# Silu through Tanh, paired value blocks and a detached last linear in a two-block macaron kernel

## The chip, the core and the metric

The kernel runs on one core of a Trainium2 chip. The metric is the time of one execution on the device in microseconds, taken as the median of several runs. The profiles come from the hardware profiler, one execution each.

## The reference

The input x has 16 batches of 256 rows of 128 features, all float32. One feed-forward, a cheap attention, the same feed-forward again, and then a mixture of experts, a real attention and the mixture of experts again are added to x one after the other, each on the layer-normed x:

```
x = x + 0.5 * ffn(norm(x))              # which = 0
x = x + nonlocal_attention(norm(x))     # no softmax: three small products per batch
x = x + 0.5 * ffn(norm(x))              # which = 1, same weights
x = x + 0.5 * experts(norm(x))          # 2 of 8 experts of rank 64 by the first row of each batch
x = x + attention(norm(x))              # 16 heads of 8, rotary, causal, softmax
x = x + 0.5 * experts(norm(x))

ffn(x):  h = silu(x w1 * s1) * (x w2 * s2)     # 128 -> 512
         h = gelu(h h1 * s_h1)                 # 512 -> 512, exact gelu
         h = gelu(h h2 * s_h2)                 # 512 -> 512
         return h w3 * s3                      # 512 -> 128
```

## The kernel before

x stays in on-chip memory the whole time. The 16 batches form nine groups (`BATCHES`): seven of two batches and two of one. Each group passes the two feed-forwards and the attention blocks; the unit of work of a feed-forward is one group, so 512 columns for the large groups and 256 for the small ones.

**The order of work is planned when the kernel is built.** Every piece of work is a Python generator, called a line. It yields a `step` before each operation: the engine, an assumed duration, the PSUM banks and buffers it takes and drops, the results it needs. A loop at the end of the kernel keeps a clock for each engine, picks the line that can begin first, issues its operation and advances the clock. The instructions of an engine are pinned in that order (`Ordered`, the helper at line 227, so nearly all instructions carry that line in the profile). The planner runs once; on the chip each engine runs its list in order and waits on semaphores.

- `main` is the line of `feed_forwards`: it goes through `order`, in which the two feed-forwards of different groups alternate, and issues the matmuls of each with their full 128*128 tiling. While feed-forwards remain, other lines go first on TensorE when they are ready (`back`), and `main` fills the rest.
- In a feed-forward (`ffn`) the first stage makes, for each of four chunks of the 512 hidden features, one matmul with `w1T` into a bank `pu` and one with `w2T` into a bank `pw`. The line `silu` reads `pu` on ScalarE and drops the bank; `product` multiplies on VectorE with `pw` and the scale `s2` and writes `h`. The two 512 x 512 layers follow in seven block products each instead of eight (Strassen), whose operand differences `T` run on VectorE or POOL and whose sums `h<-h,pb` run on VectorE, then Gelu on ScalarE. The last linear, `w3s`, is issued by `main` itself, in two halves; after it `main` goes to the next feed-forward.
- After a feed-forward other lines are spawned: `nonlocal_attn` after the first, `experts`, `attention` and `after_attention` after the second.
- `attention` makes score blocks with four matmuls side by side in 32 rows each (tiling 32*128 in the profile, `pb<-qkv`), once for the row maxima (`maxima`, VectorE's TENSOR_REDUCE `mx`) and once for the exponentials (`weighted`). A score block takes four PSUM banks (a quad). `softmax` runs Exp on ScalarE into a buffer `pr` (three of them) and POOL zeroes what lies above the diagonal. The heads are four quarters, `j` = 0, 2, 1, 3. `values` takes one quarter at a time: 16 matmuls in the tiling 128*32 (`pb<-pr,vm`) on `pr`, which it then drops. In the last two groups (`late`) the result is given on in halves.
- The flag `ended` is set when `main` has issued the last feed-forward. From then on the planner may use all banks, adds the mask of the scores on TensorE, and puts matmuls of the identity (`pb<-ident`) into idle stretches of TensorE to keep its clock up (`awake`).
- `either` steps may run on one of two engines; `pick` takes the one that would be done first by the planner's clocks, with `SPARED` added for VectorE. `LOAN` makes the first four banks dearer, `PATIENCE` delays an exponential that needs a table load, `SLACK` is the span of time within which candidates count as equally early.

ScalarE needs a table for its functions, and the program loads another where the function needs it (ACT_TABLE_LOAD).

The scales `s1` and `s2` come in on POOL's DMA queue. The first group's layer norm (`first_input`) uses POOL for one power (`rstd`).

Of the kernel before, what the change touches and what calls it, by code (L numbers as in the profile page):

```python
# [20 lines left out]
P = 128  # L21
# [6 lines left out]
LANDING = 2.2  # L28
LOAN = 1.5
SPARED = 0.5  # L30
PATIENCE = 1.5
HURRY = 1
SLACK = 0.02
HOP = {"PE": 0.24, "ACT": 0.15, "DVE": 0.12, "POOL": 0.08}
# [23 lines left out]
def macaron_kernel(ctx: ExitStack, tc: tile.TileContext, a: dict, out: bass.AP):  # L58
# [30 lines left out]
    warm = cst.tile([P, 1], F32, name="warm")  # L89
    nc.scalar.activation(warm, ident[:, :1], AF.Silu)  # L90
    for _ in range(WARM):
        nc.tensor.matmul(pb[:, 7, :P], ident, ident, start=True, stop=True)
    s1 = load("s1", [P, KC], a["s1"], nc.gpsimd)
    s2 = load("s2", [P, KC], a["s2"], nc.gpsimd)

    rot = cst.tile([P, 4, TG], F32, name="rot")
# [278 lines left out]
    def ffn(which, t0, n):  # L375
        me, N = (which, t0), n * P
        xnT = xnTs.pop(me)
        h = None

        def silu(c, pu, sil):  # L380
            yield act(N, table="silu", drop=(pu,), sets=(("s", c, me),))
            nc.scalar.activation(sil[:, :N], pu.t[:, :N], AF.Silu, scale=s1[:, c : c + 1])

# [71 lines left out]
        for c in range(KC):  # L455
            r = yield pe(0.215 * n, banks=1, after=0.0, take=("h",) if c == 0 else ())
            h = r[1] if c == 0 else h
            pu = r[0]
            nc.tensor.matmul(pu.t[:, :N], w1T[:, c * P : (c + 1) * P], xnT.t[:, :N], start=True, stop=True)
            sil = sml.tile([P, TG], F32, name="sil", bufs=3)  # L460
            spawn(silu(c, pu, sil))
            (pw,) = yield pe(0.215 * n, banks=1, after=0.0, drop=(xnT,) if c == KC - 1 else ())
            nc.tensor.matmul(pw.t[:, :N], w2T[:, c * P : (c + 1) * P], xnT.t[:, :N], start=True, stop=True)
            spawn(product(c, pw, sil, h))
            if me == (0, 0) and c == 1:
                fold_w3()
        lo, hi = 0, 2 * P
        for l, w in ((1, h1T), (2, h2T)):
# [9 lines left out]
            for p, b, first, at, second, needs in (  # L478
# [9 lines left out]
                for o in range(2):  # L488
                    for k in range(2):
                        begins, ends = o + k == 0, o + k == 2  # L490
                        drop = ()
                        if ends and p in (5, 7, 4):
                            drop = (T[{5: 1, 7: 3, 4: 4}[p]],) + ((h,) if p == 4 else ())
                        r = yield pe(
                            0.1075 * n, banks=int(new and begins), after=0.0, take=("h",) if p == 1 and begins else (),
                            needs=needs, drop=drop, sets=(("P6", l, me),) if p == 6 and ends else (),
# [20 lines left out]
                elif p == 4:  # L517
                    spawn(other_block(l, 1, 0, bk["c"], nh))
            h = nh

        half = n // 2
        po = {}
        up, down = (0, 1, 2, 3), (2, 3, 0, 1)
        for t, ks in [(t, down) for t in range(half, n)] + [(t, up) for t in range(half)]:
            new = t in (0, half)
            last = t in (half - 1, n - 1)
            r = yield pe(
                0.225 * len(ks), banks=int(new), after=0.0, needs=tuple((2, i, t // half, me) for i in range(2)),
                drop=(h,) if t == half - 1 else (),
            )  # L530
            if new:
                po[t // half] = r[0]
            b = po[t // half]
            for k in ks:
                nc.tensor.matmul(
                    b.t[:, t % half * P : (t % half + 1) * P], h.t[:, k, t * P : (t + 1) * P], w3s[:, k, :],
                    start=(k == ks[0]), stop=(k == ks[-1]),
                )
            if last:
                spawn(residual(t // half, b))  # L540

# [10 lines left out]
    def nonlocal_attn(t0, n):  # L552
# [19 lines left out]

        gram = yield from product(0.45 * nb, None, None, "gram", (xn,))
        m = yield from product(0.22 * nb, gram, pht, "gph")
        m = yield from product(0.22 * nb, m, wgT, "eff")
        if t0 == 2 * FIRST[NG - 1]:
            spawn(for_the_mask())
        (po,) = yield pe(0.45 * nb, banks=1, drop=(xnT,))
        for t in range(n):
# [7 lines left out]
    def gated(nb, cls):  # L587

        (bk,) = yield pe(0.22 * nb, banks=1)
        pl = bk.t[:, : nb * NE].rearrange("p (b e) -> p b e", e=NE)  # L590
# [32 lines left out]
        for b in range(nb):  # L623
            scaled_by(ab.t[:, b, D:], ab.t[:, b, D:], gw[:, b : b + 1])
        (bk,) = yield pe(0.23 * nb, banks=1, drop=(ab,))
        pw = bk.t[:, : 2 * D].rearrange("p (b d) -> p b d", b=2)
# [11 lines left out]
    def applied(key, sg, xnT):  # L638
        yield step(None, 0.0, needs=(key,))
        we = merged[key]  # L640
        (po,) = yield pe(0.225 * sg.n, banks=1, drop=(we, xnT) if sg.last else (xnT,))
        for t in range(sg.n):
            nc.tensor.matmul(
                po.t[:, t * D : (t + 1) * D], xnT.t[:, t * P : (t + 1) * P], we.t[:, t // 2, :], start=True, stop=True
            )
        yield dve(sg.n * P, drop=(po,))
        add_residual(sg.t0, sg.n, po)
# [55 lines left out]
    def attention(sg):  # L703
# [6 lines left out]
        if sg.first:  # L710

            (bk,) = yield pe(0.22 * nb, banks=1)
            py = bk.t[:1, : 2 * D].rearrange("p (b d) -> p b d", b=2)
# [33 lines left out]
        spawn(queries())  # L747
        (bk,) = yield pe(0.225 * n, banks=1, needs=(("q", sg.t0),), drop=(xnT,))
        pv = bk.t.rearrange("p (t d) -> p t d", d=D)
# [75 lines left out]
        def weighted(i):  # L825
# [55 lines left out]
            def values():  # L881

                po = [None, None]
                for j in (0, 2, 1, 3):
                    new = j == 0 or (late and j == 1)
                    yield step(None, 0.0, needs=(("pr", sg.t0, i, j), ("v", sg.t0)))
                    pr = prs[j]
                    r = yield pe(0.025 + 0.00174 * o, banks=int(new), tiles="col", drop=(pr,))
                    if new:
                        po[j % 2 :] = [r[0]] * (2 - j % 2)  # L890
                    half = slice((j % 2) * w, (j % 2) * w + w)
                    pp = po[j % 2].t[:, half]
                    for k, f, at in runs:
                        for r in range(4):
                            nc.tensor.matmul(
                                pp[32 * r : 32 * r + 32, (f - q0) * P :], vm.t[:, base // P + k, r, j, :],
                                pr.t[:, r, at : at + (q1 - f) * P],
                                start=(j < 2 and k == 0), stop=(j >= 2 and k == q1 - 1), skip_group_check=True,
                            )
                    if late and j >= 2:  # L900
                        spawn(output(pp, oT[:, half], w // 32, j % 2, po[j % 2], ("oT", sg.t0, i, j)))
                    elif j == 3:
                        spawn(output(po[0].t[:, : 2 * w], oT[:, : 2 * w], w // 16, 0, po[0], ("oT", sg.t0, i, j)))
# [204 lines left out]
    def feed_forwards():  # L1108

        for which, sg in order:  # L1110
# [13 lines left out]
            if (which, sg) == order[0]:  # L1124
                fold_rest()
        ended[0] = True

# [9 lines left out]
    while lines:  # L1137
# [4 lines left out]
        back = engine == "PE" and begun[0] <= len(order) - HURRY  # L1142
        line = min(soon, key=lambda r: ((r[2] is main) == back, r[2].rank, r[1]))[2]
        issue(line)
# [71 lines left out]
```

## Time and profile before

| | |
|---|---|
| median of 3 runs | 934.62 us (934.36 to 934.98) |
| the profiled execution | 934.55 us |
| its span, first to last instruction | 932.8 us |
| mean granted TensorE clock | 0.996 |
| TensorE busy | 904.2 us (97%) |
| VectorE busy | 636.3 us (68%) |
| ScalarE busy | 471.5 us (51%), of it 110.3 us table loads |
| POOL busy | 356.4 us (38%) |
| first matmul of the first and of the last feed-forward | 8.6 and 817.5 us |
| last matmul of the last feed-forward's last linear | 845.2 us |

In a row of the profile's groups, the names left of the arrow are written and those right of it read, buffer numbers left out; `pb` is the whole of PSUM. Behind the bar stand the busy time in us, the mean of one in ns, the idle time of the engine just before these instructions, and what ended most of it. A timeline row gives start, duration and engine, and merges neighbours of one kind (x16). A float32 matmul appears as two instructions. DMA traffic matters at the start alone: the weights and x come in during the first 30 us.

### The profile page before, as it was taken

Reading aid. Unit: us, or ns where it says so; the run is one execution under the profiler, and the core shown is the slowest. Engines: PE = TensorE matmul, PEld = TensorE weight load, DVE = VectorE, ACT = ScalarE, POOL = GpSimd, SP = SyncE. Lnnn points to the kernel's source line nnn. Section 1 sums busy time; section 2 is a strip of 40 time slices with the busy share of each in tenths; the row PEclk is TensorE's granted clock in tenths of the full one; section 3 lists DMA queues with packets and bytes.
Section 4 is the critical chain, followed back from the end, with each engine's and each line's share of the span. In section 5 each row is a group of like instructions: output and inputs, shape, how many; then the busy total and the mean of one; then the engine's idle time right before and its main releaser. Section 6 shows DMA issues by size and latency. Waiting matters only on the chain.

```text
span 932.8 us, 16458 instructions
## 1 busy us (share of the span) xinstructions
PE 904.2 (97%) x6524; PEld 680.5 (73%) x6524; DVE 636.3 (68%) x1474; ACT 471.5 (51%) x691; POOL 356.4 (38%) x537
## 2 busy tenths in 40 slices
PE   6999999999999999999999999999999989999998
PEld 4778778686786767787677767866786767877666
DVE  4744646875488485894678764894778586977773
ACT  2233533645754646546555466547574657465332
POOL 5311313522454334442453324532463246443441
PEclk9999999999999999999999999999999999999999
DMA  8100000000000000000000000000000000000000
GB/s 240 33 1 1 1 1 12 12 1 1 13 12 12 1 2 12 24 1 1 12 1 24 1 1 13 24 1 1 13 2 23 1 12 1 25 7 2 13 19 12
DMA packets 14588, 13.68 MB, mean 15 GB/s; under 512 B 2032, under 2 KB 11952, under 8 KB 14512
## 3 DMA queue, kind: packets, MB, share of 16 engines
q1 hardware_dynamic: 12496, 8.04, 3.0%
q0 software_dynamic: 1600, 4.20, 1.6%
q8 instruction: 51, 0.84, 0.4%
q10 hardware_dynamic: 416, 0.39, 0.1%
q14 instruction: 25, 0.20, 0.1%
HBM read 10.53 MB, written 2.10 MB: 14 GB/s over the span
## 4 chain that ended last, share of the span: by engine, by line
PE 70%; DVE 14%; ACT 6%; issue 4%; POOL 2%; DMA 2%; SPq 1%; POOLq 0%; DVEq 0%
PE pb L227 70%; DVE mx L227 4%; DVE h L227 3%; ACT L227 2%; ACT pr L227 2%; DVE pb L227 2%; DMA w3s<-in_w3T_dram 1%; ACT h L227 1%; POOL pr L227 1%; DVE T L227 1%; DMA x<-in_x_dram 1%; DVE st L227 1%; DVE qkv L227 1%; POOL rstd L227 1%; DVE row L227 0%
## 5 line engine op out<-in xcount | busy, mean ns | idle before, releaser
L227 DVE TENSOR_TENSOR h<-h,pb 128x512 f32<-128x512 f32 (+1 forms) x180 | 111.7, 620 | 80.8 <-PE pb L227 78.8
L227 PE MATMUL pb<-T,hS 128*128 128x256 f32 (+1 forms) x576 | 131.8, 364 | 3.9 <-DVE h L227 2.8
L227 POOL TENSOR_SCALAR_AFFINE_SELECT pr<-pr 128x512 f32<-128x512 f32 x128 | 78.8, 639 | 140.4 <-ACT pr L227 135.3
L227 ACT ACTIVATE h<-h 128x512 f32<-128x512 f32 (+1 forms) x108 | 62.3, 581 | 137.7 <-DVE h L227 137.3
L227 ACT ACTIVATE pr<-pb 128x1536 f32<-128x1536 f32 x64 | 92.7, 1449 | 54.0 <-PE pb L227 40.4
L227 PE MATMUL pb<-qkv 32*128 32x256 f32 (+2 forms) x1536 | 115.2, 406 | 4.7 <-ACT pr L227 2.5
L227 ACT ACT_TABLE_LOAD x86 | 110.3, 1283 | 17.8 <-PE pb L227 15.5
L227 DVE TENSOR_REDUCE mx<-pb 128x8 f32<-128x2048 f32 (+1 forms) x64 | 111.9, 1750 | 6.1 <-PE pb L227 5.7
L227 PEld LDWEIGHTS pb<-T,hS 128*128 128x128 f32 x576 | 96.5, 190 | 21.1 <-issue 8.6
L227 DVE TENSOR_TENSOR pb<-pb,causal 128x1024 f32<-128x1024 f32 x56 | 68.7, 1226 | 45.4 <-PE pb L227 37.3
L227 PEld LDWEIGHTS pb<-qkv 32*128 32x128 f32 x1536 | 68.0, 184 | 38.3 <-issue 11.4
L227 ACT ACTIVATE xn<-x,shift,rstd 128x128 f32<-128x128 f32 x138 | 57.1, 482 | 52.9 <-POOL shift L227 52.7
L227 POOL TENSOR_SCALAR nm<-mv 128x4 f32<-128x4 f32 (+3 forms) x56 | 14.8, 264 | 168.3 <-DVE mv L227 167.1
L227 POOL TENSOR_TENSOR T<-h 128x512 f32<-128x512 f32 (+1 forms) x48 | 53.4, 1112 | 58.9 <-ACT h L227 54.9
L227 POOL TENSOR_TENSOR T<-h,T 128x512 f32<-128x512 f32 (+1 forms) x40 | 46.1, 1151 | 64.9 <-DVE h L227 35.0
L227 PE MATMUL pb<-xnT,w1T 128*128 128x512 f32 (+1 forms) x144 | 68.9, 560 | 0.9 <-ACT xnT L227 0.9
L227 PE MATMUL pb<-xnT,w2T 128*128 128x512 f32 (+1 forms) x144 | 68.2, 555 | 1.0 <-ACT sil L227 0.8
L227 PE MATMUL pb<-h,h1T 128*128 128x256 f32 (+1 forms) x288 | 68.8, 364 | 0.0
L227 POOL TENSOR_TENSOR rstd<-ve,mhalf 128x4 f32<-128x4 f32 (+3 forms) x63 | 58.9, 935 | 24.9 <-DVE ve L227 20.1
L227 PE MATMUL pb<-h,h2T 128*128 128x256 f32 (+1 forms) x288 | 67.1, 364 | 0.0
L227 PE MATMUL pb<-T,h1T 128*128 128x256 f32 (+1 forms) x288 | 66.1, 359 | 0.0
L227 PEld LDWEIGHTS pb<-w3s,h 128*128 128x128 f32 x512 | 60.6, 192 | 7.0 <-issue 6.0
(138 smaller groups left out, 1568.9 us busy)
## 6 DMA issues: line engine op xcount, KB each, us to landing
out_dram<-x SPq DMA_DIRECT2D x7, 256.0 KB, 2.3
x<-in_x_dram SPq DMA_DIRECT2D x6, 256.0 KB, 5.3
h1T<-in_h1T_dram SPq DMA_DIRECT2D x1, 1024.0 KB, 9.6
h2T<-in_h2T_dram SPq DMA_DIRECT2D x1, 1024.0 KB, 11.0
ab<-in_eab_dram,at POOLq DMA_INDIRECT x32, 2.9
x<-in_x_dram SPq DMA_DIRECT2D x3, 128.0 KB, 5.4
w1T<-in_w1T_dram SPq DMA_DIRECT2D x1, 256.0 KB, 3.5
w2T<-in_w2T_dram ACTq DMA_DIRECT2D x1, 256.0 KB, 3.9
```

The lines of the kernel that those rows point to most:

```text
L227: return lambda *args, **kw: tc.keep_in_program_order(getattr(self.engine, name)(*args, **kw))
```

## The change

Silu(u) is computed as u (1 + tanh(u / 2)) / 2. The two halves are put into the scales: `s1` is halved and `s2` multiplied by the halved `s1`, on POOL, after their load. ScalarE writes Tanh of the scaled bank, and a new VectorE operation makes (tanh + 1) times the bank; the bank is dropped after that. The planner counts Tanh to Gelu's table, and the first table loaded is Gelu's.

`values` takes the quarters 0 and 2 in one step and 1 and 3 in another, but for late groups. The last linear becomes a line of its own with the rank of `main`; `main` goes on, and sets `ended` when the last feed-forward's residuals are added. While TensorE is in one of the tilings, candidates of a tiling go before untiled ones. The planner's assumed times of TensorE and five of its constants change.

```
-LOAN = 1.5
-SPARED = 0.5
-PATIENCE = 1.5
+LOAN = 2.0
+SPARED = 0.1
+PATIENCE = 1
-SLACK = 0.02
+SLACK = 0.05
...
-    nc.scalar.activation(warm, ident[:, :1], AF.Silu)
+    nc.scalar.activation(warm, ident[:, :1], AF.Gelu)
...
     s1 = load("s1", [P, KC], a["s1"], nc.gpsimd)
     s2 = load("s2", [P, KC], a["s2"], nc.gpsimd)
+    nc.gpsimd.tensor_scalar(s1, s1, 0.5, None, ALU.mult)
+    nc.gpsimd.tensor_tensor(s2, s2, s1, ALU.mult)
...
         def silu(c, pu, sil):
-            yield act(N, table="silu", drop=(pu,), sets=(("s", c, me),))
-            nc.scalar.activation(sil[:, :N], pu.t[:, :N], AF.Silu, scale=s1[:, c : c + 1])
+            yield act(N, table=soft)
+            nc.scalar.activation(sil[:, :N], pu.t[:, :N], AF.Tanh, scale=s1[:, c : c + 1])
+            yield dve(N, drop=(pu,), sets=(("s", c, me),))
+            nc.vector.scalar_tensor_tensor(sil[:, :N], sil[:, :N], 1.0, pu.t[:, :N], ALU.add, ALU.mult)
...
-            r = yield pe(0.215 * n, banks=1, after=0.0, take=("h",) if c == 0 else ())
+            r = yield pe(0.015 + 0.215 * n, banks=1, after=0.0, take=("h",) if c == 0 else ())
...
-        half = n // 2
+        def last_linear(h=h):
...
-            r = yield pe(
-                0.225 * len(ks), banks=int(new), after=0.0, needs=tuple((2, i, t // half, me) for i in range(2)),
+                r = yield pe(
+                    0.237 * len(ks), banks=int(new), after=0.0, needs=tuple((2, i, t // half, me) for i in range(2)),
...
+        spawn(last_linear(), since=0.0)
...
-                for j in (0, 2, 1, 3):
-                    new = j == 0 or (late and j == 1)
-                    yield step(None, 0.0, needs=(("pr", sg.t0, i, j), ("v", sg.t0)))
-                    pr = prs[j]
-                    r = yield pe(0.025 + 0.00174 * o, banks=int(new), tiles="col", drop=(pr,))
+                for js in ((0,), (2,), (1,), (3,)) if late else ((0, 2), (1, 3)):
+                    new = js[0] == 0 or (late and js[0] == 1)
+                    yield step(None, 0.0, needs=tuple(("pr", sg.t0, i, j) for j in js) + (("v", sg.t0),))
+                    r = yield pe(
+                        (0.025 + 0.00174 * o) * len(js), banks=int(new), tiles="col", drop=tuple(prs[j] for j in js)
+                    )
...
+        yield step(None, 0.0, needs=tuple(("ffn", h, (1, order[-1][1].t0)) for h in range(2)))
         ended[0] = True
...
-        line = min(soon, key=lambda r: ((r[2] is main) == back, r[2].rank, r[1]))[2]
+        inside = engine == "PE" and tiles[0] is not None
+        line = min(
+            soon, key=lambda r: (inside and r[2].next["tiles"] is None, (r[2] is main) == back, r[2].rank, r[1])
+        )[2]
```

The other changed lines set the assumed time of a 128-column matmul pair to 0.237 us (from 0.22 to 0.23) and add 0.015 us to each step of the feed-forward.

## The prediction

> **What bounds the kernel now.** I read the busy rows of the page first, then the table of stretches, then the waits of TensorE inside one stretch, and last the timeline, since a share of 97% does not say whether the rest can be had.
>
> ```profile
> PE 904.2 (97%) x6524; PEld 680.5 (73%) x6524; DVE 636.3 (68%) x1474; ACT 471.5 (51%) x691; POOL 356.4 (38%) x537
> ...
> L227 ACT ACT_TABLE_LOAD x86 | 110.3, 1283 | 17.8 <-PE pb L227 15.5
> ```
>
> Busy time in stretches of one period of the steady schedule (two batches through all blocks), and the whole list of TensorE's waits in the second of them:
>
> ```profile
> core 0: us, PE busy (x) PEld busy (x) DVE busy (x) ACT busy (x) POOL busy (x), PEclk, DMA share, GB/s
> 282.00:390.00 108.00, 107.82 (x755) 78.39 (x754) 75.70 (x171) 59.19 (x83) 43.35 (x62) 1.00 0.03 8
> 390.00:498.00 108.00, 107.82 (x755) 78.47 (x754) 75.73 (x171) 59.18 (x83) 43.36 (x62) 1.00 0.03 9
> ...
> PE pb L227 <- ACT pr L227: 0.2, 1, 0.2
> ```
>
> TensorE is busy 107.82 of 108.00 us at full clock and waits once, for 0.2 us. VectorE has 32 us free in a period, ScalarE 49. So faster ScalarE or shorter chains win nothing here; only less TensorE time does. The timeline shows TensorE time that is no arithmetic:
>
> ```profile
> 460.33 0.70 PE L227 MATMUL pb<-T,hS 128*128 128x256 f32 x2
> 460.96 0.86 PE L227 MATMUL pb<-pr,vm 128*32 128x256 f32 x16
> 461.74 0.70 PE L227 MATMUL pb<-T,hS 128*128 128x256 f32 x2
> 462.37 0.94 PE L227 MATMUL pb<-qkv 32*128 32x256 f32 x16
> ...
> 474.31 1.89 PE L227 MATMUL pb<-h,h2T 128*128 128x256 f32 x8
> 476.04 1.89 PE L227 MATMUL pb<-T,h2T 128*128 128x256 f32 x8
> ```
>
> From start to start, eight 128x256 instructions take 476.04 - 474.31 = 1.73 us, 0.43 a pair. A pair between two blocks in another tiling (128*32 for values, 32*128 for scores) takes 460.96 - 460.33 = 0.63: 0.20 more. The value block takes 461.74 - 460.96 = 0.78; its 8 instructions of 256 and 8 of 128 columns, four side by side at 0.213 and 0.107 us each, would stream in 0.64. So a value block costs about 0.34 us beyond its arithmetic. A period has 22 tiled blocks (14 of scores, 8 of values).
>
> **The change, part by part.** Durations are of the profiled execution, 934.55 us (span 932.8 and 1.75 around it); the median of the runs, 934.62, differs by 0.07.
>
> *Values of two quarters in one step.* The 14 batches of the seven groups that are not late have two value blocks instead of four: 28 blocks fewer. The two ends of a block (0.20) certainly go; of the 0.14 inside, the part at its end (the profile has no two value blocks side by side) may or may not. Bounds 28 x 0.20 = 5.6 and 28 x 0.34 = 9.5; I take 0.30, nearer the row: **-8.4**. This is on the path, since TensorE is full. The pair now waits for the later of two softmaxes and holds two of three `pr` buffers longer; queued behind on TensorE is whatever was planned next, and the row blocks 2.9 us apart leave time for it. Without that cover it is one late row block a batch.
>
> *Tiled work preferred while TensorE is tiled.* A value block right after a score block saves the 0.20 of one pair. Before the last feed-forward all score blocks use one set of four banks that must be read out first, so two score blocks rarely meet. I guess ten meetings in the whole run: **-2** (0 to -6).
>
> *Silu as tanh with one more VectorE pass.* 56 of 512 and 16 of 256 columns. The nearest row is the product that already runs there with the same operation and operands:
>
> ```profile
> L227 DVE SCALAR_TENSOR_TENSOR h<-pb,s,sil 128x512 f32<-128x512 f32 x56 | 41.3, 743 | 12.1 <-PE pb L227 8.2 <-ACT sil L227 3.7
> L227 DVE SCALAR_TENSOR_TENSOR h<-pb,s,sil 128x256 f32<-128x256 f32 x16 | 7.3, 478 | 4.7 <-ACT sil L227 4.7
> ```
>
> So 41.3 + 7.3 = 49 us more on VectorE, 685 of 933 (73%); in a period two feed-forwards, 8 x 0.74 = 5.9, 82 of 108. Average room covers it; a burst may not:
>
> ```profile
> 436.00:456.00 20.00, 20.00 (x132) 13.71 (x131) 19.31 (x40) 7.50 (x14) 4.91 (x7) 1.00 0.01 2
> ```
>
> Around the first stage of one feed-forward of each period VectorE (third figure) is busy 19.31 of 20 us with the maxima of the attention. 4 x 0.74 = 3.0 us come in there. The product, the later sums and the maxima queue behind each new pass, and the bank of the first linear is now held until that pass, not until the ACTIVATE. Other TensorE work covers a late sum, and VectorE is idle again a few us later. From 0 to 3.0 in each of some 14 larger feed-forwards (0 to 42 us); I take **+1**, by the row that shows TensorE not waiting through a full burst. The lower price asked of VectorE (SPARED) moves some scalings and copies to it as well; that has the same cover and the same bounds.
>
> The table loads go the other way, and here a rule speaks against the change:
>
> ```profile
> 494.46 0.29 ACT L227 ACTIVATE ew<-wt,sel 128x2 f32<-128x2 f32 x1 [1.75 <-DVE wt L227]
> 495.06 0.63 ACT L227 ACTIVATE h<-h 128x512 f32<-128x512 f32 x1 [0.30 <-DVE h L227]
> 495.71 1.28 ACT L227 ACT_TABLE_LOAD   x1
> 499.02 0.69 ACT L227 ACTIVATE sil<-pb,s 128x512 f32<-128x512 f32 x1 [2.03 <-PE pb L227]
> ```
>
> `ew` is a Tanh; the Gelu `h` after it has no load between. The Trainium skill, ScalarE: Activation LUTs, section "Table sets: the hidden batching unit", lists tanh with the sets of exp and sigmoid and not with that of gelu. By the page each Silu group would still pay its loads, and none goes; by the row Tanh runs under Gelu's table, and in today's order of ScalarE the Silu groups melt into Gelu's: 58 loads for 87, 29 x 1.28 = 37 us less. I go by the row. As ScalarE is idle half the time, this is 0 on the path in the steady part, and at most the waits left elsewhere (below).
>
> *The two scales on POOL at the start.* Two small POOL operations, about 0.25 us each (row `shift`, 217 ns), but POOL runs in order and they wait for `s1` and `s2`:
>
> ```profile
> 1.39 0.75 POOL L76 DMA_DIRECT2D s<-in_s_dram  x1 [0.35 <-issue]
> 2.50 0.59 POOL L76 DMA_DIRECT2D s<-in_s_dram  x1
> 5.11 1.03 POOL L227 TENSOR_TENSOR rstd<-ve,mhalf 128x4 f32<-128x4 f32 x1 [2.02 <-DVE ve L227]
> ...
> s<-in_s_dram POOLq DMA_DIRECT2D x2, 2.0 KB, 7.7
> ```
>
> They land 7.7 us after issue, at 9.1 and 10.2. The first `rstd` is queued behind, and all else of the first input behind it: it moves from 5.1 to about 10.6, the first linear from 8.6 to about 14.2. Most of that is hidden: today TensorE stands still from 12.3 to 16.8 for the second input, whose DMA lands at 12.7, and then runs the next matmuls at half clock. I put two chunks of the first linear into that hole. What is left is the four new VectorE passes where VectorE also scales weights: **+2.5** (0 to 5.6).
>
> *Last linear as its own line, later `ended`, new costs in the planner.* No instruction is added. Each feed-forward's last matmuls may run after the next one's first. In the steady part there is no wait to remove, so 0. From 606 to 846 TensorE is idle 240 - 231.34 = 8.7 us and after 846 9.6, the latter between score blocks that VectorE and ScalarE hold up, filled with idle matmuls. A new order of issue can win or lose a few us there; bounds -9 and +6, I take 0. No DMA is moved but for the input scales' readers.
>
> Sum: 934.55 - 8.4 - 2 + 1 + 2.5 = 927.65, say **928**.
>
> **Rivals.**
> (a) *Order gains too.* Fewer loads and freer last linears remove half of the 8.7 and 9.6 us of idle TensorE after 606: 928 - 9 = 919. For it: table loads stand in the chain that ended last around 734 to 749. Against: most of the tail is VectorE's maxima, which stay.
> (b) *The start is not hidden and little else is won* (slow clock, start 5.6, values 5.6, nothing from `inside`): 934.55 - 5.6 + 5.6 = 934.6, no change.
> (c) *VectorE becomes the bound in the bursts: slower.* Place: first stage of the feed-forward that meets the maxima, and the VectorE-heavy stretch 714 to 830 (90 of 116 us busy). Price: if of the 3.0 us 1.1 a feed-forward reaches TensorE in 14 of them, +15, less the forecast's +1: 928 + 14 = 942; it decides from (934.55 - 928) / 14 = 0.5 us each on top. For it: the bank held longer. Against: the burst shows no TensorE wait now.
> (d) *Tanh and Gelu do not share a table*, as the page would have it: loads stay or rise, but off the path; with later exponentials +5: 933, or slower.
>
> **Chances.** Forecast 0.43, (a) 0.21, (b) 0.11, (c) 0.21, (d) 0.04. A measurement of this kernel can tell 0.2% (1.9 us) from no change. (a) and the forecast are faster; (b) no change; (c) slower; (d) is split. Faster 0.65, same 0.12, slower 0.23. The range from 915 to 940 holds (a) with its lower bound, the forecast, (b) and (d), and about half of (c). As cases of both signs hold much, the forecast's own range from its bounds is 921 to 933.
>
> **What would show it.** Right: a period of some 106.5 us instead of 108.0, still without TensorE waits; 32 instructions in a value block of 1.4 us or so; near 58 table loads; VectorE near 685. The first linear near 14, the first Strassen products 2 to 3 us late. Wrong: waits of TensorE on VectorE `h`, `T` or `sil` in the period (then c), a period that is unchanged (the merged block pays its switches inside), 87 loads or more (d), or a tail after the last feed-forward that differs from 87 us by more than 3.

## The result: 945.7 us for 934.5, and the profile after

The changed kernel takes 945.67 us (944.45 to 949.47, four runs) and the kernel before, in the same rounds, 934.49 us. The ratio is 1.0127, with a 95% interval of 1.0107 to 1.0147: slower, where 928 was forecast. The profiled execution took 944.45 us, its span is 942.7.

The busy row of the page, and of its groups the table loads:

```profile
PE 897.6 (95%) x6492; PEld 679.7 (72%) x6492; DVE 716.0 (76%) x1636; ACT 412.6 (44%) x613; POOL 312.0 (33%) x498
...
L229 ACT ACT_TABLE_LOAD x57 | 73.1, 1283 | 6.8 <-DVE mx L229 5.3
```

Fifty-eight loads for 87, as foreseen (one more stands at the warm-up). VectorE has 80 us more, not 49. The new pass is 37.6 + 6.3 = 44 of them; the other 36 are steps that came over from ScalarE and POOL, and nearly as much (35 us) goes back when SPARED alone is set back (a_spared below). The groups of the new pass and of the layer norm's scaling, the latter 36 times on VectorE before:

```profile
L229 DVE SCALAR_TENSOR_TENSOR sil<-sil,pb 128x512 f32<-128x512 f32 x56 | 37.6, 678 | 10.4 <-ACT sil L229 10.4
L229 DVE SCALAR_TENSOR_TENSOR sil<-sil,pb 128x256 f32<-128x256 f32 x16 | 6.3, 410 | 4.2 <-ACT sil L229 4.1
L229 DVE TENSOR_SCALAR xn<-x,rstd,shift 128x128 f32<-128x128 f32 x76 | 27.8, 426 | 5.1 <-POOL shift L229 5.0
```

Two periods of the steady schedule by stretches, and the waits of TensorE in the first of them (us in total, times, longest):

```profile
core 0: us, PE busy (x) PEld busy (x) DVE busy (x) ACT busy (x) POOL busy (x), PEclk, DMA share, GB/s
396.30:505.90 109.60, 107.36 (x755) 78.89 (x754) 89.97 (x202) 47.62 (x64) 34.60 (x55) 1.00 0.03 8
505.90:615.40 109.50, 107.27 (x754) 78.78 (x754) 89.85 (x202) 47.63 (x64) 34.60 (x55) 1.00 0.03 8
...
PE pb L229 <- DVE mx L229: 1.3, 2, 1.1
PE pb L229 <- DVE xnT L229: 0.8, 1, 0.8
```

A period takes 109.5 us where it took 108.0, and TensorE stands where it did not stand before. The two places in the timeline of TensorE, each with the VectorE rows that belong to it, and at the end the first place as the kernel before has it (in brackets the idle time ahead of a row, and what ended it):

```profile
434.51 1.14 PE L229 MATMUL pb<-qkv 32*128 32x512 f32 x8
435.58 0.70 PE L229 MATMUL pb<-T,hS 128*128 128x256 f32 x2
436.21 1.51 PE L229 MATMUL pb<-pr,vm 128*32 128x256 f32 x32
437.65 0.70 PE L229 MATMUL pb<-T,hS 128*128 128x256 f32 x2
439.40 1.15 PE L229 MATMUL pb<-qkv 32*128 32x256 f32 x16 [1.05 <-DVE mx L229]
...
435.79 1.23 DVE L229 TENSOR_TENSOR pb<-pb,causal 128x1024 f32<-128x1024 f32 x1 [4.13 <-PE pb L229]
437.05 2.29 DVE L229 TENSOR_REDUCE mx<-pb 128x8 f32<-128x2048 f32 x1
...
461.52 0.61 PE L229 MATMUL pb<-wrT,xnT 128*128 128x8 f32 x4 [0.78 <-DVE xnT L229]
...
460.77 0.69 DVE L229 COPY xnT<-pb 128x512 f32<-128x512 f32 x1 [1.97 <-PE pb L229]
...
434.57 1.14 PE L227 MATMUL pb<-qkv 32*128 32x512 f32 x8
437.58 2.28 DVE L227 TENSOR_REDUCE mx<-pb 128x8 f32<-128x2048 f32 x1
440.76 1.15 PE L227 MATMUL pb<-qkv 32*128 32x256 f32 x16
```

The joined value block is there: 437.65 - 436.21 = 1.44 us for two quarters, and 0.20 in the pair before it, 1.64 where two blocks cost 2 x (0.78 + 0.20) = 1.96. That is 0.32 saved. But the next score block waits 1.05 us for the maxima to be read out of its four banks. VectorE is not late there from load: it had stood idle for 4.13 us before it began on this score block, and the mask (1.23 us) and the maxima (2.29) follow at once. In the kernel before the like two score blocks start 440.76 - 434.57 = 6.19 us apart, with other matmuls between, and the maxima are done first. In the new order they start 439.40 - 434.51 = 4.89 us apart, the wait included. At 461.5 TensorE waits for a copy on VectorE, and VectorE itself had stood 1.97 us waiting for TensorE. Both waits come from the order of the lists, not from a VectorE that is too busy.

Where the time went, by the start of the first linear of the feed-forwards and the start of the last matmul of the last linear (from the traces):

| us | before | after | difference |
|---|---|---|---|
| first feed-forward | 8.6 | 14.4 | +5.8 |
| second | 53.8 | 55.1 | +1.3 |
| seventh | 282.0 | 285.8 | +3.8 |
| ninth | 390.0 | 396.4 | +6.4 |
| thirteenth | 606.0 | 615.5 | +9.5 |
| last linear's last matmul | 845.2 | 858.4 | +13.2 |
| span | 932.8 | 942.7 | +9.9 |

All of it is lost before the last feed-forward ends, most of it from the fifth feed-forward on; the stretch after it is 3 us shorter.

### The profile page after: what moved, and what is told of

Read it like the earlier page. It is cut to its first block, busy times and chain, and to the rows that moved or that the text cites. A ratio compares the mean times of both kernels' runs of the same rounds, so it can differ in the third digit from the quotient of the medians.

```text
span 942.7 us, 16380 instructions
## 1 busy us (share of the span) xinstructions
PE 897.6 (95%) x6492; PEld 679.7 (72%) x6492; DVE 716.0 (76%) x1636; ACT 412.6 (44%) x613; POOL 312.0 (33%) x498
## 4 chain that ended last, share of the span: by engine, by line
PE 63%; DVE 20%; ACT 6%; issue 5%; POOL 3%; DMA 2%; SPq 1%; POOLq 0%; DVEq 0%; ACTq 0%
PE pb L229 63%; DVE mx L229 5%; DVE pb L229 3%; DVE h L229 3%; ACT L229 2%; ACT pr L229 2%; DMA w3s<-in_w3T_dram 1%; DVE sil L229 1%; DVE st L229 1%; DVE rot L229 1%; POOL pr L229 1%; POOL rstd L229 1%; DVE T L229 1%; DVE x L229 1%; ACT xn L229 1%
## 5 line engine op out<-in xcount | busy, mean ns | idle before, releaser
L229 PEld LDWEIGHTS pb<-T,hS 128*128 128x128 f32 x576 | 96.6, 190 | 26.4 <-issue 7.5
L229 ACT ACTIVATE sil<-pb,s 128x512 f32<-128x512 f32 (+1 forms) x72 | 45.0, 633 | 60.5 <-PE pb L229 60.0
L229 POOL TENSOR_TENSOR rstd<-ve,mhalf 128x4 f32<-128x4 f32 (+3 forms) x63 | 61.8, 981 | 21.5 <-DVE ve L229 16.9
L229 DVE TENSOR_TENSOR x<-x,pb 128x256 f32<-128x256 f32 (+2 forms) x79 | 37.2, 471 | 40.9 <-PE pb L229 40.8
L229 PE MATMUL pb<-T,h2T 128*128 128x256 f32 (+1 forms) x288 | 66.6, 362 | 1.4 <-POOL T L229 1.3
L229 PE MATMUL pb<-h,h1T 128*128 128x256 f32 (+1 forms) x288 | 66.6, 362 | 0.0
L229 PE MATMUL pb<-h,h2T 128*128 128x256 f32 (+1 forms) x288 | 64.8, 361 | 0.0
## 6 DMA issues: line engine op xcount, KB each, us to landing
h2T<-in_h2T_dram SPq DMA_DIRECT2D x1, 1024.0 KB, 10.7
```

Source lines behind the costliest of these rows:

```text
L229: return lambda *args, **kw: tc.keep_in_program_order(getattr(self.engine, name)(*args, **kw))
```

## Experiments

Each label names what it starts from: b_ is the kernel before with something done to it, a_ the changed kernel. Ratios are to the kernel before in the same rounds, with 95% intervals.

| | us | ratio |
|---|---|---|
| b_pair | 937.26 | 1.0020 (1.0012 to 1.0029) |
| b_tanh | 961.48 | 1.0279 (1.0258 to 1.0300) |
| b_tanh_plan | 966.26 | 1.0341 (1.0315 to 1.0368) |
| a_spared | 945.08 | 1.0103 (1.0082 to 1.0124) |
| b_load | 974.15 | 1.0421 (1.0404 to 1.0439) |
| b_free | 981.44 | 1.0500 (1.0482 to 1.0518) |
| a_silu | 945.05 | 1.0126 (1.0094 to 1.0159) |
| b_line | 953.82 | 1.0208 (1.0191 to 1.0225) |
| a_oldnum | 951.99 | 1.0178 (1.0157 to 1.0199) |
| a_peold | 953.57 | 1.0200 (1.0174 to 1.0227) |
| a_const | 951.86 | 1.0170 (1.0148 to 1.0193) |
| b_num | 968.80 | 1.0379 (1.0305 to 1.0453) |
| a_nopass | 936.32 | 1.0013 (1.0005 to 1.0022) |
| a_silu_plan | 952.58 | 1.0186 (1.0165 to 1.0207) |
| b_pair_plan | 942.78 | 1.0081 (1.0060 to 1.0102) |
| b_slack | 956.80 | 1.0226 (1.0197 to 1.0255) |
| b_pair5 | 937.93 | 1.0032 (1.0021 to 1.0044) |
| b_pair6 | 938.75 | 1.0039 (1.0025 to 1.0052) |

### The parts one by one

**b_pair**, the paired values alone:

```
-                for j in (0, 2, 1, 3):
+                for js in ((0,), (2,), (1,), (3,)) if late else ((0, 2), (1, 3)):
...
```

> The kernel before with one part of the change: values of quarters 0 and 2, 1 and 3 in one step (not in the late groups). Theory V (VectorE is the cause of the loss, the paired value blocks do save TensorE time): 28 value blocks fewer at 0.30 us, about 926 us, the steady period near 106.8 us with no TensorE wait. Rival P (the paired blocks themselves cost: they hold two of three pr buffers and wait for the later softmax): no faster than before, 934 or more, with TensorE waiting for ACT pr or POOL pr in the period.

```profile
334.20:441.40 107.20, 106.77 (x756) 79.09 (x752) 76.96 (x173) 64.20 (x87) 41.42 (x61) 1.00 0.03 8
843.60:935.30 91.70, 79.33 (x844) 59.00 (x843) 58.66 (x158) 29.58 (x37) 31.54 (x50) 0.96 0.04 11
```

These are stretches of b_pair: one period, and what follows its last feed-forward. The period is 107.1 to 107.2 us, 0.8 to 0.9 shorter, so pairing does save TensorE time. The end takes 91.7 us where it took 86.9, with a granted clock of 0.96 there for 0.98, and the total is 0.2% above the kernel before. Neither theory had that.

**b_tanh**, Tanh with the VectorE pass and the scales on POOL, planned anew with all numbers as before (and Gelu's table loaded first):

```
+    nc.gpsimd.tensor_scalar(s1, s1, 0.5, None, ALU.mult)
+    nc.gpsimd.tensor_tensor(s2, s2, s1, ALU.mult)
...
-            yield act(N, table="silu", drop=(pu,), sets=(("s", c, me),))
-            nc.scalar.activation(sil[:, :N], pu.t[:, :N], AF.Silu, scale=s1[:, c : c + 1])
+            yield act(N, table=soft)
+            nc.scalar.activation(sil[:, :N], pu.t[:, :N], AF.Tanh, scale=s1[:, c : c + 1])
+            yield dve(N, drop=(pu,), sets=(("s", c, me),))
+            nc.vector.scalar_tensor_tensor(sil[:, :N], sil[:, :N], 1.0, pu.t[:, :N], ALU.add, ALU.mult)
```

> The kernel before with one part of the change: Silu from Tanh with the additional VectorE pass, the scales combined on POOL at the start, and the planner told of both. All constants as before. Theory V: 49 us more on VectorE is enough to make TensorE wait; period 109 to 110 us, total 942 to 950. Rival O (the constants and the order of issue are the cause): period 108.0 to 108.3, total 934 to 938, the difference only at the start.

It is 26.4 us slower than the kernel before, more than twice what the whole change costs, and outside both ranges.

**b_line**, the last linear as its own line, the later `ended` and the tiled preference:

```
-        half = n // 2
+        def last_linear(h=h):
...
+        spawn(last_linear(), since=0.0)
...
+        yield step(None, 0.0, needs=tuple(("ffn", h, (1, order[-1][1].t0)) for h in range(2)))
         ended[0] = True
...
-        line = min(soon, key=lambda r: ((r[2] is main) == back, r[2].rank, r[1]))[2]
+        inside = engine == "PE" and tiles[0] is not None
...
```

> The kernel before with the last linear as its own line, the later ended and the preference for tiled work while TensorE is tiled; nothing else. Theory of the prediction: no wait to remove in the period, so 108.0 us again, total 930 to 937. If the freer last linear is worth something: period under 107.5, total under 930. If it lets other work fall behind: over 938, with a longer stretch after the last feed-forward.

```profile
506.00:616.80 110.80, 107.81 (x754) 78.47 (x753) 82.59 (x180) 60.36 (x80) 39.61 (x60) 1.00 0.03 8
...
PE pb L227 <- DVE mx L227: 1.2, 2, 0.8
PE pb L227 <- DVE h L227: 0.9, 1, 0.9
PE pb L227 <- DVE xn L227: 0.9, 1, 0.9
```

A stretch and its TensorE waits. No arithmetic is added, and it costs 19.3 us: the new order gives VectorE 82.6 us a period, from 75.7, and TensorE waits 3 us. The stretch after the last feed-forward, which was to show work falling behind, is no more than 1 us longer.

**a_silu**, the changed kernel with Silu back and planned so:

```
-            nc.scalar.activation(sil[:, :N], pu.t[:, :N], AF.Tanh, scale=s1[:, c : c + 1])
-            yield dve(N, drop=(pu,), sets=(("s", c, me),))
-            nc.vector.scalar_tensor_tensor(sil[:, :N], sil[:, :N], 1.0, pu.t[:, :N], ALU.add, ALU.mult)
+            nc.scalar.activation(sil[:, :N], pu.t[:, :N], AF.Silu, scale=s1[:, c : c + 1])
...
```

> The changed kernel with Silu back as one ScalarE operation (its own table, scales as loaded, no additional VectorE pass); paired values, the last linear as its own line, constants and assumed times as changed. If the VectorE pass is the whole loss: at or under the kernel before, 920 to 934, with a period near 107. If the rest of the change costs too: 938 or more.

At 945.05 it is as slow as the changed kernel. The VectorE pass is not the whole loss. By this pair of kernels the trade of Silu for Tanh and a pass costs nothing, by b_tanh 26 us, and in both pairs the order changes with it. The parts do not add.

### Load in a fixed order

For these the planner is not told, so every engine keeps its order of issue, and an added operation stands in its engine's list right behind the place of the Silu.

**b_tanh_plan**, the order before, with Tanh and the pass put in, and the scales and the first table as in b_tanh:

```
             yield act(N, table="silu", drop=(pu,), sets=(("s", c, me),))
-            nc.scalar.activation(sil[:, :N], pu.t[:, :N], AF.Silu, scale=s1[:, c : c + 1])
+            nc.scalar.activation(sil[:, :N], pu.t[:, :N], AF.Tanh, scale=s1[:, c : c + 1])
+            nc.vector.scalar_tensor_tensor(sil[:, :N], sil[:, :N], 1.0, pu.t[:, :N], ALU.add, ALU.mult)
```

> As the former, but the planner is not told: every engine keeps the order of issue of the kernel before, and the additional VectorE pass is put right behind the Tanh of its chunk. So only the load on the engines differs. Theory V in its plain form (time on VectorE counts, wherever it is put): about as slow as with the planner told, 942 or more. If the order made by the planner is what costs: 935 to 939, TensorE waits in the period under 0.5 us.

Slower by 31.2 us. The waits of TensorE over the whole run, then the timeline of a burst, with VectorE and TensorE rows:

```profile
PE pb L229 <- DVE sil L229: 15.0, 24, 1.9
PE pb L229 <- DVE mx L229: 9.2, 12, 1.2
...
461.27 0.87 DVE L229 BATCH_NORM_STATS2 st<-x 128x6 f32<-128x128 f32 x4
462.83 0.69 DVE L229 SCALAR_TENSOR_TENSOR sil<-sil,pb 128x512 f32<-128x512 f32 x1 [0.42 <-ACT sil L229]
463.57 1.13 PE L229 MATMUL pb<-xnT,w1T 128*128 128x512 f32 x2 [0.64 <-DVE sil L229]
...
466.22 0.68 DVE L229 SCALAR_TENSOR_TENSOR sil<-sil,pb 128x512 f32<-128x512 f32 x1
467.67 1.22 DVE L229 TENSOR_REDUCE mx<-pb 128x8 f32<-128x1024 f32 x1
468.94 0.44 PE L229 MATMUL pb<-ident,mx 128*128 128x128 f32 x2 [1.23 <-DVE mx L229]
```

Two mechanisms show: a first linear waits for the bank that the pass still reads (0.64), and the maxima come late, with passes ahead of them in VectorE's list (1.23).

**b_free** starts from b_tanh_plan and takes the first away: ScalarE copies the bank into the `h` chunk, and the pass reads that.

```
+            nc.scalar.copy(h.t[:, c, :N], pu.t[:, :N])
+            nc.vector.scalar_tensor_tensor(sil[:, :N], sil[:, :N], 1.0, h.t[:, c, :N], ALU.add, ALU.mult)
```

> b_tanh_plan with one more ScalarE operation: a copy of the bank into the h chunk that product overwrites later, read by the additional VectorE pass instead of the bank. So the bank is free after ScalarE, the VectorE passes stay in number, place and chain, and ScalarE gets about 42 us more. Theory B: TensorE waits for DVE sil go from 15 us to about 0 and the total falls by 12 us or more from 966, to 954 or less. Theory L: it stays within 5 us of 966.

No wait for `sil` is left in TensorE's list, and it takes 981.44 us, 15 more; neither theory had that. With the bank free TensorE waits elsewhere. What the bank alone costs is not shown: the copies also load ScalarE, and VectorE now stands 25.0 us ahead of its passes, waiting for the copies, where it stood 12.3 us in b_tanh_plan.

**b_load** adds a pass that nobody reads, with Silu as before:

```
             nc.scalar.activation(sil[:, :N], pu.t[:, :N], AF.Silu, scale=s1[:, c : c + 1])
+            nc.vector.scalar_tensor_tensor(more[:, :N], sil[:, :N], 1.0, sil[:, :N], ALU.add, ALU.mult)
```

> The kernel before with Silu as it was, and one more VectorE pass of the same size at the place of the additional pass, which reads the finished sil and writes a tile that nobody reads; the planner is not told. VectorE gets the same 49 us, but no bank is held and nothing waits for the result. Theory L (load: the passes delay whatever is queued behind them on VectorE): most of the 31 us of b_tanh_plan, 955 to 965, with TensorE waiting for DVE mx, h and T. Theory B (bank: the bank of the first linear is held until the pass, so the first linear of the chunk after next waits): at most a third of it, 936 to 945.

```profile
405.40:518.80 113.40, 109.46 (x755) 78.38 (x754) 81.35 (x179) 59.33 (x83) 43.67 (x62) 1.00 0.03 8
...
PE pb L227 <- DVE h L227: 10.1, 15, 2.5
PE pb L227 <- DVE mx L227: 10.0, 14, 1.2
PE pb L227 <- ACT xn L227: 6.9, 5, 4.3
...
DVE more L227 <- ACT sil L227: 19.6, 22, 2.4
```

The stretch of one period, the longest of TensorE's waits over the run, and VectorE's own wait ahead of the pass. VectorE goes from 75.7 to 81.4 us of 113.4, still 32 us free, and the period is 5.4 us longer: about as much as the 5.7 us of added passes. The total rises by 39.6 us, more than theory L said. So in this order added VectorE work costs without a bank held and without anybody reading its result. It is not load alone: the pass stands where `sil` may not be ready, and VectorE then stands too. In the period quoted that is 0.9 us, over the run 19.6, where VectorE stood 8.4 us for `sil` in the kernel before.

**a_nopass** is the reverse in the changed kernel's order, the 72 passes left out:

```
             yield dve(N, drop=(pu,), sets=(("s", c, me),))
-            nc.vector.scalar_tensor_tensor(sil[:, :N], sil[:, :N], 1.0, pu.t[:, :N], ALU.add, ALU.mult)
```

> The changed kernel with its order of issue untouched and the 72 additional VectorE passes left out (so what product multiplies is the bare Tanh, not Silu). Theory L (in a fixed order the passes delay what is queued behind them): 49 us less on VectorE give back 10 us or more, 925 to 936. Theory O (the order costs, whatever the load): 940 to 946.

**a_silu_plan** has Silu in the place of Tanh there:

```
-            nc.scalar.activation(sil[:, :N], pu.t[:, :N], AF.Tanh, scale=s1[:, c : c + 1])
+            nc.scalar.activation(sil[:, :N], pu.t[:, :N], AF.Silu, scale=s1[:, c : c + 1])
...
-            nc.vector.scalar_tensor_tensor(sil[:, :N], sil[:, :N], 1.0, pu.t[:, :N], ALU.add, ALU.mult)
```

> The changed kernel's order with Silu as one ScalarE operation in the place of Tanh and no VectorE pass; the planner still counts the pass and one table. ScalarE gets its Silu table loads back, about 37 us. Theory L: 928 to 940, a few us above a_nopass. Theory O: 942 to 948.

Without the pass 936.32, 9.4 us less than the changed kernel: here, where the planner chose its place, it costs a quarter of what b_load's pass costs. A period of a_nopass with its TensorE waits, then a wait of the changed kernel over its whole run that a_nopass does not have:

```profile
391.90:501.00 109.10, 106.86 (x754) 78.73 (x753) 84.87 (x194) 47.61 (x64) 34.59 (x55) 1.00 0.03 8
...
PE pb L229 <- DVE mx L229: 1.3, 2, 1.1
PE pb L229 <- DVE xnT L229: 0.8, 1, 0.8
...
PE pb L229 <- DVE sil L229: 5.3, 6, 1.8
```

In the steady period the pass costs 0.4 us of 109.5. The same two waits stay without it, with VectorE 5 us less busy, so the 1.1 us that remain over 108.0 are the order's, with the saved switches already in it. By the starts of the feed-forwards the pass costs 1.4 us before the second, 3.9 from there to the thirteenth, 3.1 from there to the last linear and 0.8 behind it. TensorE never reads `sil`; it waits for the bank that the pass still holds, 5.3 us over the run, and not at all in a_nopass.

With Silu in that order the run takes 952.58, outside both ranges. The table loads of ScalarE in a_nopass and in a_silu_plan:

```profile
L229 ACT ACT_TABLE_LOAD x57 | 73.1, 1283 | 6.6 <-DVE mx L229 5.3 <-DVE oT L229 0.3
...
L227 ACT ACT_TABLE_LOAD x106 | 136.0, 1283 | 19.6 <-PE pb L227 12.2 <-DVE mx L227 5.3 <-DVE oT L227 0.3
```

In an order made for one table, Silu costs 49 loads, 63 us of ScalarE, and the run is 16.3 us longer. In this order the trade of Silu for Tanh and a pass gains 7 us; in the order before it loses 31. In both, the operations that the order was planned with are the faster ones.

### The planner's numbers

**a_spared** sets one constant back:

```
-SPARED = 0.1
+SPARED = 0.5
```

> The changed kernel with SPARED back at 0.5, so that steps that may run on either of two engines go to VectorE less often. Theory V: VectorE falls from 716 us toward 690, and 3 to 8 us of the loss come back, 938 to 942. Rival O: the total stays within 2 us of the changed kernel's 945.7, or moves without relation to the busy time of VectorE.

VectorE falls from 716.0 to 680.9 us and the time stays, 945.08: the rival's case. That the moved steps cost nothing is not shown, since the order is made anew here too.

**a_oldnum** has all three parts with the numbers of before, **a_peold** the old assumed times of TensorE (the last two lines and others like them), **a_const** the old constants, which are four, not five:

```
-LOAN = 2.0
-SPARED = 0.1
-PATIENCE = 1
+LOAN = 1.5
+SPARED = 0.5
+PATIENCE = 1.5
...
-SLACK = 0.05
+SLACK = 0.02
...
-            r = yield pe(0.015 + 0.215 * n, banks=1, after=0.0, take=("h",) if c == 0 else ())
+            r = yield pe(0.215 * n, banks=1, after=0.0, take=("h",) if c == 0 else ())
...
```

> The three parts of the change (Tanh with the VectorE pass, paired values, last linear as its own line with the tiled preference) with all of the planner's numbers as before: the four constants and the assumed times of TensorE. Theory N (the parts cost about 27, 2 and 19 us, and the new numbers give most of it back): 965 to 985. Theory M (the parts do not add up, since all run into the same VectorE bursts): 945 to 960.

> The changed kernel with the assumed times of TensorE as before, the four constants as changed. Theory T (assuming TensorE about 3% slower makes the planner leave VectorE more room behind each step, so that its real, longer operations are in time): clearly slower than the changed kernel, 955 or more. If the constants are what gives back: within 3 us of 945.7.

> The changed kernel with the four constants as before (LOAN, SPARED, PATIENCE, SLACK), the assumed times of TensorE as changed. Theory T: 943 to 950. If the constants are what gives back: 955 or more.

They take 951.99, 953.57 and 951.86 us; the last two fall between their ranges. Both halves of the new numbers are needed for the last 6 to 8 us, and neither alone does anything: the theory that a slower assumed TensorE leaves VectorE room is not borne out (a_const has it and is no better than a_oldnum).

**b_num** gives the kernel before the new numbers alone, **b_slack** one of them:

```
-SLACK = 0.02
+SLACK = 0.05
```

> The kernel before with the planner's new numbers alone: the four constants and the assumed times of TensorE. The order of the kernel before has no TensorE wait in its period, so new numbers can only keep or lose that: 934 to 945, with VectorE above 636 us because SPARED is lower. A gain under 930 would mean that the numbers alone are worth something.

> The kernel before with SLACK 0.05 for 0.02 and nothing else: no work is added or taken, only candidates within 0.05 us count as equally early. Theory O (the order of the kernel before is one that happens to leave TensorE without waits, and nearly any other order loses that): 940 to 965, with TensorE waits on VectorE in the period. Against it: 933 to 937.

b_num takes 968.80 us (965.86 to 979.61 in four runs), far over its range, b_slack 956.80. In b_slack the same arithmetic is done, in another order; VectorE is busy 11 us more over the run, POOL as long as before, and there are 94 table loads for 87. Two of its stretches, the first shorter than a period, TensorE's waits from 228 to 408 us, and the longest wait in the first stretch with what follows it:

```profile
347.90:407.80 59.90, 57.14 (x375) 41.16 (x373) 43.37 (x109) 31.84 (x44) 24.90 (x36) 0.97 0.05 14
407.80:518.90 111.10, 109.08 (x757) 78.84 (x753) 80.29 (x175) 62.92 (x84) 41.90 (x61) 1.00 0.03 8
...
PE pb L227 <- DVE h L227: 2.9, 3, 1.8
PE pb L227 <- DVE cls L227: 1.9, 1, 1.9
PE pb L227 <- DVE mx L227: 1.9, 2, 1.7
...
389.15 0.61 PE L227 MATMUL pb<-wrT,cls 128*128 128x8 f32 x4 [1.94 <-DVE cls L227]
389.62 4.38 PE L227 MATMUL pb<-T,hS 128*128 128x256 f32 x12
```

One constant of the planner, with no arithmetic added, costs 21.5 us, nearly twice as much as the change. TensorE waits for VectorE again. After the 1.94 us for `cls` twelve matmuls take 4.38 us, where twelve of the same take 2.75 in the kernel before (at 407.3 us), and the granted clock of that stretch is 0.97. Over the run it is 0.990 for 0.996: by these two figures some 5 of the 21.5 us are clock (an estimate).

### Can the saved switches be kept?

**b_pair_plan** joins the values in the order before, by issuing the first quarter where the second stands (one pair of 28 excepted, whose buffer is taken again too early):

```
+                    held.append(j)
+                    for i2 in () if j < 2 and not late and (sg.t0, i, j) not in SINGLE else held:
...
```

> The kernel before in its own order of issue on every engine, but the values of quarter 0 (and 1) are issued where those of quarter 2 (and 3) stand, so 27 value blocks are joined to the next; one pair is left apart. The planner is not told. If joining saves the switches and nothing else moves: 27 x 0.21 to 0.30 us less, 926.5 to 929, the first version faster than the kernel before. If the later start of the first half delays others: 934 or more.

942.78 us: worse. Rows of its timeline at the place that the prediction quotes of the kernel before:

```profile
462.85 0.94 PE L228 MATMUL pb<-qkv 32*128 32x256 f32 x16 [0.19 <-ACT pr L228]
463.71 1.13 PE L228 MATMUL pb<-T,hS 128*128 128x256 f32 x4
465.35 0.94 PE L228 MATMUL pb<-qkv 32*128 32x256 f32 x16 [0.51 <-ACT pr L228]
...
463.85 1.45 ACT L228 ACTIVATE pr<-pb 128x1536 f32<-128x1536 f32 x1 [1.05 <-PE pb L228]
```

The next score block needs the banks that the exponential (1.45 us) is reading. Before, a value block and two pairs filled that time; with the value block gone two pairs do not, and TensorE stands 0.51 us. The block was cover. Over the run these waits for `pr` come to 12.7 us, 21 times, where they were 4.2 us, 9 times.

**b_pair5** and **b_pair6** pair in the first five or six groups alone (`sg.g >= 6` in the second):

```
-                for js in ((0,), (2,), (1,), (3,)) if late else ((0, 2), (1, 3)):
+                for js in ((0,), (2,), (1,), (3,)) if sg.g >= 5 else ((0, 2), (1, 3)):
```

> b_pair with paired values in the first five groups alone (20 value blocks fewer, not 28). If the pairs of groups 5 and 6 make the tail long: period 107.1 and the tail of the kernel before, 930 to 932. If the tail comes from the new order: 934 to 945.

> b_pair with paired values in the first six groups alone (24 value blocks fewer); the last large group, whose attention still runs after the last feed-forward, takes its quarters one by one. If its pairs make the tail long: 929 to 932. If the tail comes from the new order: 934 to 945.

937.93 and 938.75. Both have the short period (b_pair5: first linears at 281.1, 388.3 and 495.4), and both end late. The pairs of the last groups are not the reason; by the either-or of the expectation it is the new order, for which no single wait is shown. In b_pair5 the last linear is done 4.6 us earlier than in the kernel before, and the stretch behind it is 8.1 us longer. No version here beats the kernel before.

## Why the prediction was wrong

- **The step that failed is "No instruction is added ... In the steady part there is no wait to remove, so 0", with bounds of -9 and +6 for a new order of issue.** That there was no wait to remove was right. But where there is none, a new order can only add some, and it did: b_slack loses 21.5 us, b_line 19.3, b_num 33.4, with no arithmetic added, all far outside the bound. In the changed kernel itself the period is 109.5 us for the 106.5 that was said, and 109.1 with the pass left out. Without the pass the sum forecasts -7.9 us; a_nopass measures +1.0 against the kernel before in its rounds. That puts about 9 us on the new order, with whatever the tiled preference and the pairs did in it.
- **The VectorE pass, +1, was mis-sized: it is 9.4 us in the changed order (a_nopass).** In the order before it is 31, with the start and the fewer loads in it (b_tanh_plan). I argued from a 73% busy engine and a burst without a wait; b_load shows a period growing by about the length of the passes while VectorE has 32 us of it free. The lists are in order and fixed: work that could fill the gap stands behind the instruction that waits. The pass was priced at 49 us and takes 44. The 36 us of other steps that came to VectorE were not sized.
- **Table loads, "0 on the path", are not settled.** The 16 us of a_silu_plan are the price of 49 loads in an order planned without them; no run takes the loads alone out of the order before, which is what the term was about. The count of 58 came out, partly by luck: it was made for the order before, where Tanh leaves 56 (b_tanh_plan), and other orders have 50 to 62. Tanh under Gelu's table was right: the row showed it, and the list of the Trainium skill, ScalarE: Activation LUTs, section "Table sets: the hidden batching unit", did not.
- **The saved switches, -8.4, were right in size and not in effect.** The 0.213 and 0.107 us of that sum follow from the trace, where 512, 256 and 128 columns take 592, 379 and 273 ns: 213 ns for 256 columns more, 106 for 128. A block saves 0.32 us in the changed kernel's timeline, for 0.30 forecast; b_pair's period is 0.85 us shorter of 4 x 0.32 = 1.3. In the fixed order they turn into waits for the exponential.
- **The tiled preference, -2, shows no gain**; it was not tried by itself.
- **The start, +2.5, came out at 1.3**: `rstd` at 10.7 (10.6 said), first linear at 14.4 (14.2 said), second feed-forward 1.3 us later. Without the passes it begins at 53.7, as before: the wait for the scales is hidden, and what is left is the passes, as was said.
- Rival (c), VectorE in the bursts, had the right sign and its 942 is nearest; its cause was only part of it. The bank held longer is there: TensorE waits 5.3 us for `sil` over the run. But in the period quoted above it waits for the maxima of scores and a copy, and those waits stay without the pass.

What stays open: why the order before has no waits, and whether a planner with other numbers would find one like it for the new operations; each setting was tried once. No single quantity of the runs explains the totals; VectorE's busy time does not (716 us and 945.7, 683 and 974, 648 and 957). The parts of b_line were not tried one by one, nor was a planner with the measured durations of VectorE.

## What to carry to other kernels

Where a static order already keeps the bounding engine without waits, an edit that makes the order anew can lose more than it saves: the kernels made anew from this one took 0.2 to 3.8% longer. A forecast needs a term for that, and an edit's own worth is seen by putting it into the old order and into the new. The idle share of a second engine, 32% of VectorE here, is no measure of what more work on it costs: what counts is what stands behind each operation in its list, and how much other work a list has between two operations of which one waits for the other. And a block taken from the bounding engine may have been the cover for another engine's latency, as the value blocks were for the exponentials.

## What the runs showed that was not expected

A pass on VectorE that nothing reads, 0.68 us at the median and 72 times, costs 39.6 us of a run in which VectorE is 70% busy. Put into an order planned without them, 63 us of table loads on an engine that is half idle cost 16 us. And the longest wait in the period of the changed kernel is for an engine that had just stood idle for 4 us.
